# Loading, turning and projecting the first row tile ahead of its chunk in a local-attention and expert-layer kernel

## The chip, the core and the metric

The kernel runs on one core of one Trainium2 chip. The metric is device time in microseconds (us), the median of the runs shown; smaller is better. TensorE is written PE below, VectorE DVE, ScalarE ACT, GpSimd POOL and SyncE SP.

## The reference

There are 4096 rows (2 batches of 2048) of 256 features. The part that the change touches is the attention of the first layer, 16 heads of 16 features, each row seeing itself and the 64 rows before it:

```python
qkv = x @ W_attn + b_attn
q, k, v = jnp.split(qkv, 3, axis=-1)        # 16 heads of 16
scores = jnp.einsum('bhtd,bhsd->bhts', q, k) * scale
mask = causal & (j >= i - 64)
attn = jax.nn.softmax(jnp.where(mask, scores, -jnp.inf), axis=-1)
out = jnp.einsum('bhts,bhsd->bhtd', attn, v)
x1 = layernorm(x + out @ W_proj + b_proj)
...
# then: a router picks one of 8 experts for each row (256 -> 1024, gelu),
# a shared second layer (1024 -> 256), two layernorms
```

## The kernel before

**Tiles, chunks and steps.** A row tile is 128 rows; there are 32, and attention takes one in each step `i` of `for i in range(NT)`. Four tiles make a chunk (`CH` = 512 rows, `TPC` = 4), and there are 8 chunks. The input projection works on whole chunks. A piece of it is named by the triple (chunk, piece, part): piece 0 turns the rows of `xts[c]` by PE transposes into `axT[c]`, with features on the partitions; piece 1 makes the queries, piece 2 the keys, piece 3 the values. Each piece has two parts. `project` issues a part's PE work into a PSUM tile of the pool `ps_m` (tag `pm`, two buffers in turn), and `keep` copies it out and thereby frees the buffer. A part of piece 1 or 2 is two fp32 products of 512 columns, which the profile shows as four PE instructions; a part of piece 3 is eight instructions of 256 columns in two halves.

**What copies what.** In `keep`, part 0 of the turned rows goes by ACT, part 1 by DVE. Part 0 of the queries is copied twice, by ACT (L468) and then by DVE (L476), since two variants of the queries are stored; part 1 twice by DVE (L473, L476). Part 0 of the keys goes by ACT (L482), part 1 by DVE (L487). Values go by DVE (L492) and then by DMAs into the shifted copy `vh` (L503 to L513).

**Before the loop.** SP's queue issues the loads in order: the first chunk's rows (512 KB), the bias rows `bst`, three column blocks of `wa` (queries, keys, values; 256 KB each), and smaller ones; then the second chunk's rows. While they land, PE runs 16 transposes (L391), and DVE and POOL make masks and constants. Then pieces 0, 1 and 2 of chunk 0 are projected and kept, part by part.

**Step 0** is written out by hand: the scores of tile 0 (masks L526, 64 small products L538), four row maxima on DVE (L550), two of the four groups of exponentials on ACT (`exps`, L554), then the parts (0,3,0), (0,3,1), (1,0,0), (1,0,1) projected and kept, then the other two groups of exponentials, and then (1,1,0) and (1,1,1), the second chunk's queries.

**Later steps** run four tiles in different stages: scores of tile `i`, transposes of the probabilities of `i-1` (L609, copied by ACT L615 and DVE L617), `weigh` (L629), normalisation and output projection (`join`, L660) of the tile before, and layernorm of the one before that. `scores(i)` writes four PSUM banks `s0` to `s3`, each of which becomes free when the exponentials of that bank in step `i-1` are done. Two slots of each step (`work[i]`) take one part each of the next chunk's projection from a list, `line`. In steps 1 and 3 one part is split into its halves and fills both slots; step 2 has the turning of chunk 2's part 0 and one part from the list.

**Order.** From the first projection on, the engines are in `manual_schedule`: every engine runs its instructions in the order of the program text. What stands ahead of that is ordered by the framework's scheduler. `turned` gives two PSUM banks in turn (pool `ps_t`) for transposed tiles. After the loop come the expert blocks, with products L222 and L242, which the change leaves alone.

Of the kernel before, what the change touches and what calls it, by code (L numbers as in the profile page):

```python
# [10 lines left out]
F32 = mybir.dt.float32  # L11
BF16 = mybir.dt.bfloat16
I32 = mybir.dt.int32
AF = mybir.ActivationFunctionType
ALU = mybir.AluOpType
AX = mybir.AxisListType

P = 128
CTX = 64
HD = 16  # L20
CH = 512
TPC = CH // P
# [11 lines left out]
def kernel(  # L34
# [16 lines left out]
    nc = tc.nc  # L51
    B, T, C = x.shape
    E, _, FF = w1.shape
    KC = C // P
    NH = C // HD
    NT = B * T // P
# [14 lines left out]
    xf = x.rearrange("b t c -> (b t) c")  # L71
# [8 lines left out]
    ident = const.tile([P, P], F32, name="ident")  # L80
# [40 lines left out]
    def turned(name):  # L121

        turns.append(name)
        return ps_t.tile([P, 4, P], F32, tag=f"pt{len(turns) % 2}", name=name)
# [160 lines left out]
    with ExitStack() as att:  # L285
        aw = att.enter_context(tc.tile_pool(name="aw", bufs=1))
        xp = att.enter_context(tc.tile_pool(name="xp", bufs=2))
        p2 = att.enter_context(tc.tile_pool(name="p2", bufs=2))
        small = att.enter_context(tc.tile_pool(name="small", bufs=4))
        def load_x(c):  # L290
            xt = xp.tile([P, TPC, C], F32, tag="xt", name=f"xt_{c}")
            nc.sync.dma_start(
                out=xt, in_=xf[ts(c, CH), :].rearrange("(j p) c -> p j c", p=P)
            )
            return xt

        xts = {0: load_x(0)}
        bst = aw.tile([3 * KC, P], F32, name="bst")
        nc.sync.dma_start(out=bst, in_=b_attn.rearrange("(g p) -> g p", p=P))
        wa = aw.tile([P, KC, 3 * C], F32, name="wa")  # L300
        wav = w_attn.rearrange("(k p) f -> p k f", p=P)
        for n in range(3):
            nc.sync.dma_start(out=wa[:, :, ts(n, C)], in_=wav[:, :, ts(n, C)])
        bv_bc = aw.tile([P, C], F32, name="bv_bc")
        nc.sync.dma_start(out=bv_bc, in_=b_attn[2 * C : 3 * C].partition_broadcast(P))
        wrs = aw.tile([E, C], F32, name="wrs")
# [11 lines left out]
        def load_rest():  # L318
            nc.sync.dma_start(out=wpj, in_=w_proj.rearrange("(k p) f -> p k f", p=P))
            nc.sync.dma_start(out=bp_bc, in_=b_proj.partition_broadcast(P))  # L320
# [20 lines left out]
        half = aw.tile([P, 2], F32, name="half")  # L341
# [52 lines left out]
        bqkv = aw.tile([P, 3 * KC], F32, name="bqkv")  # L394
# [8 lines left out]
        qs, ks, vs, vh, xbs, axT, x1s, x1Ts, pxs = {}, {}, {}, {}, {}, {}, {}, {}, {}  # L403
# [3 lines left out]
        def project(c, piece, part, halves=(0, 1)):  # L407


            if (c, piece, part) not in pxs:  # L410
                pxs[c, piece, part] = psum(f"pj_{c}_{piece}_{part}")
            pm = pxs[c, piece, part]
            if piece == 0:
                for j in range(TPC):
                    nc.tensor.transpose(pm[:, ts(j, P)], xts[c][:, j, ts(part, P)], ident)
            elif piece in (1, 2):
                f = (piece - 1) * KC + part
                for k in halves:
                    nc.tensor.matmul(  # L419
                        pm, lhsT=wa[:, k, ts(f, P)], rhs=axT[c][:, k, :],  # L420
                        start=(k == 0), stop=(k == KC - 1),
                    )
            else:
                for a in halves:
                    for k in range(KC):
                        nc.tensor.matmul(  # L426
                            pm[:, ts(a, C)],
                            lhsT=axT[c][:, k, ts(2 * part + a, P)],
                            rhs=wa[:, k, 2 * C : 3 * C],
                            start=(k == 0), stop=(k == KC - 1),  # L430
                        )
# [23 lines left out]
                if first:  # L455
                    nc.gpsimd.memset(vh[c][0:CTX, 0].rearrange("p m s d -> p (m s d)"), 0.0)

        def keep(c, piece, part, halves=(0, 1)):
            pm = pxs.pop((c, piece, part))
            if piece == 0:  # L460
                if part == 0:
                    nc.scalar.copy(axT[c][:, part, :], pm)
                else:
                    nc.vector.tensor_copy(axT[c][:, part, :], pm)
            elif piece == 1:
                bias = bqkv[:, part : part + 1]
                if part == 0:
                    nc.scalar.activation(  # L468
                        qs[c][:, part, 1, :], pm, AF.Identity,
                        bias=bq1[:, part : part + 1], scale=half[:, 1:2],  # L470
                    )
                else:
                    nc.vector.tensor_scalar(  # L473
                        qs[c][:, part, 1, :], pm, bias, half[:, 1:2], ALU.add, ALU.mult
                    )
                nc.vector.tensor_scalar(  # L476
                    qs[c][:, part, 0, :], pm, bias, half[:, 0:1], ALU.add, ALU.mult
                )
            elif piece == 2:
                f = KC + part  # L480
                if part == 0:
                    nc.scalar.activation(  # L482
                        ks[c][:, part, CTX : CTX + CH], pm, AF.Identity,
                        bias=bqkv[:, f : f + 1], scale=1.0,
                    )
                else:
                    nc.vector.tensor_scalar(  # L487
                        ks[c][:, part, CTX : CTX + CH], pm, bqkv[:, f : f + 1], None, ALU.add
                    )
            else:  # L490
                for a in halves:
                    nc.vector.tensor_tensor(  # L492
                        vs[c][:, 2 * part + a, :, 0::2, :],
                        pm[:, ts(a, C)].rearrange("p (m s d) -> p m s d", s=2, d=HD),
                        bv_bc.rearrange("p (m s d) -> p m s d", s=2, d=HD),
                        ALU.add,
                    )
                if halves[-1] == 0:
                    return
                v, h = vs[c], vh[c]  # L500
                row = "p j m s d -> p j (m s d)"
                if part == 0 and c % (TPB // TPC) > 0:
                    nc.sync.dma_start(  # L503
                        out=h[low, 0].rearrange("p m s d -> p (m s d)"),
                        in_=vs[c - 1][high, TPC - 1].rearrange("p m s d -> p (m s d)"),
                    )
                t0, t1 = 2 * part, 2 * part + 2
                t2 = min(t1 + 1, TPC)
                nc.sync.dma_start(
                    out=h[low, t0 + 1 : t2].rearrange(row),  # L510
                    in_=v[high, t0 : t2 - 1].rearrange(row),
                )
                nc.sync.dma_start(  # L513
                    out=h[high, t0:t1].rearrange(row), in_=v[low, t0:t1].rearrange(row)
                )
# [598 lines left out]
            )  # L1114

        xts[1] = load_x(1)
        for n in range(3):
            prepare(0, n)
            for part in range(2):
                project(0, n, part)  # L1120
                keep(0, n, part)
            if n == 0:
                load_rest()

        def quick_sums(i, r):

# [9 lines left out]
        parts = []  # L1136
        for c in range(1, NT // TPC):
            parts += [(c, n, p) for n in range(1, TPC) for p in range(2)]
            if c > 1:
                parts[-5:-3] = parts[-4], parts[-5]  # L1140
        line = iter(parts[2:])

        def whole():
            return next(line) + ((0, 1),)
# [2 lines left out]
        for i in range(1, NT - 1):  # L1147
            c = i // TPC + (1 if i % TPC == 0 else 2)
            if i % 2 == 0 and c < NT // TPC:
                work[i] = [(c, 0, 0 if i % TPC else 1, (0, 1)), whole()]  # L1150
            elif i == NT - TPC - 4:
                work[i] = [None, whole()]
            elif i in (1, 3) or NT - 6 <= i < NT - 3:
                one = next(line)
                work[i] = [one + ((0,),), one + ((1,),)]
            elif i == NT - 3:
                one = next(line)
                work[i][1], work[i + 1][1] = one + ((0,), True), one + ((1,), True)
            elif i < NT - 3:
                work[i] = [whole(), whole()]  # L1160
# [40 lines left out]
        for i in range(NT):  # L1201
# [10 lines left out]
            if i == 0:  # L1212
                consts = routing_constants()
                for r in range(1, 4):
                    row_max(t, r)
                for r in range(2):
                    exps(t, r)
                for n in ((0, 3), (1, 0), (1, 1)):
                    prepare(*n)
                for part in ((0, 3, 0), (0, 3, 1), (1, 0, 0), (1, 0, 1)):  # L1220
                    project(*part)
                    keep(*part)
                add_bias(0)
                xts[2] = load_x(2)
                for r in range(2, 4):
                    exps(t, r)
                for part in parts[:2]:
                    project(*part)
                    keep(*part)
                for pair in range(2):  # L1230
                    fold(t, pair)
                continue
# [40 lines left out]
            if i >= TPC - 1 and i % TPC in (0, TPC - 1):  # L1273
                c = (i + 1) // TPC
# [302 lines left out]
```

## Time and profile before

| | |
|---|---|
| median of 3 runs | 584.7 us (584.68 to 584.93) |
| the profiled execution | 585.55 us, of which the span of instructions is 583.7 us |
| granted PE clock, mean | 0.992 |
| PE busy | 555.0 us, 95% of the span |
| DVE, ACT, POOL busy | 402.4, 301.6, 408.0 us |
| first small product of the scores (L538) in step 0, 1, 2 | 16.45, 26.97, 35.16 us |
| the same in step 3, 4, 5 | 43.40, 51.40, 59.85 us |

The busy figures are of one execution and run over stages with different limits. A row of a timeline gives start, duration, engine, line, output and inputs, the count of merged instructions, and in brackets the engine's idle time before it with what ended it. "x8" on a product counts instructions, and a product's record holds the time from its issue to its last result, so that neighbours overlap.

### The profile page before, as it was taken

Reading aid. Unit: us, or ns where it says so; the run is one execution under the profiler, and the core shown is the slowest. Engines: PE = TensorE matmul, PEld = TensorE weight load, DVE = VectorE, ACT = ScalarE, POOL = GpSimd, SP = SyncE. Lnnn points to the kernel's source line nnn. Section 1 sums busy time; section 2 is a strip of 40 time slices with the busy share of each in tenths; the row PEclk is TensorE's granted clock in tenths of the full one; section 3 lists DMA queues with packets and bytes.
Section 4 is the critical chain, followed back from the end, with each engine's and each line's share of the span. In section 5 each row is a group of like instructions: output and inputs, shape, how many; then the busy total and the mean of one; then the engine's idle time right before and its main releaser. Section 6 shows DMA issues by size and latency. Waiting matters only on the chain.

```text
span 583.7 us, 18527 instructions
## 1 busy us (share of the span) xinstructions
PE 555.0 (95%) x7312; PEld 452.0 (77%) x7312; DVE 402.4 (69%) x966; ACT 301.6 (52%) x1005; POOL 408.0 (70%) x603
## 2 busy tenths in 40 slices
PE   8999999999999999999898999999999999999990
PEld 5658667676776767766666898999999999999880
DVE  5659788888988889989877567887863332232582
ACT  2487675776758577576765433233335455455100
POOL 5359777677787887868973488887878677652483
PEclk9999999999999999999999999999999999999996
DMA  5201603012030120211334454555555757754010
GB/s 162 86 2 46 177 25 96 21 45 79 11 104 21 46 76 12 56 30 58 90 105 127 165 181 172 182 182 181 181 194 188 261 180 246 252 160 153 19 39 27
DMA packets 35605, 64.79 MB, mean 111 GB/s; under 512 B 8558, under 2 KB 23484, under 8 KB 35516
## 3 DMA queue, kind: packets, MB, share of 16 engines
q1 hardware_dynamic: 32444, 55.19, 29.6%
q0 software_dynamic: 3072, 8.39, 4.5%
q8 instruction: 59, 0.97, 0.7%
q14 instruction: 30, 0.25, 0.1%
HBM read 48.93 MB, written 8.39 MB: 98 GB/s over the span
## 4 chain that ended last, share of the span: by engine, by line
PE 60%; POOL 14%; DVE 10%; ACT 6%; issue 3%; DMA 1%; POOLq 0%; DVEq 0%; ACTq 0%
PE ph L222 16%; PE py L242 14%; PE pt L609 6%; PE pj L419 4%; ACT pr L554 4%; PE pa L629 4%; PE py L660 4%; PE s L538 3%; POOL fd L574 3%; POOL fd L566 2%; PE pj L426 2%; DVE nm L550 2%; POOL row L849 2%; PE s L526 2%; POOL out_dram L274 1%
## 5 line engine op out<-in xcount | busy, mean ns | idle before, releaser
L554 ACT ACTIVATE pr<-s,nm 128x128 f32<-128x128 f32 x512 | 142.2, 416 | 6.9 <-DVE nm L550 5.9
L566 POOL TENSOR_TENSOR fd<-pr 128x512 f32<-128x512 f32 x62 | 79.0, 1274 | 64.6 <-ACT pr L554 64.6
L233 ACT ACTIVATE gT<-ph,bc 128x128 f32<-128x128 f32 x200 | 57.2, 370 | 107.5 <-issue 59.2
L222 PEld LDWEIGHTS ph<-xgT,wb 128*128 128x128 f32 x800 | 93.5, 192 | 1.3
L222 PE MATMUL ph<-xgT,wb 128*128 128x128 f32 x800 | 94.4, 275 | 0.0
L242 PE MATMUL py<-wo_sb,gT 128*128 128x256 f32 x400 | 90.6, 380 | 0.0
L550 DVE TENSOR_REDUCE nm<-s 128x4 f32<-128x512 f32 x128 | 82.0, 680 | 5.8 <-PE s L538 5.5
L574 POOL TENSOR_TENSOR fd<-fd 128x512 f32<-128x512 f32 (+2 forms) x93 | 76.3, 820 | 7.3
L242 PEld LDWEIGHTS py<-wo_sb,gT 128*128 128x128 f32 x400 | 74.1, 190 | 9.0
L609 PE MATMUL pt<-ident,pr 128*128 128x128 f32 x512 | 72.4, 281 | 3.8 <-DVE pT L617 1.6
L615 ACT COPY pT<-pt 128x512 f32<-128x512 f32 x64 | 38.5, 601 | 69.3 <-DVE nm L550 27.3
L609 PEld LDWEIGHTS pt<-ident,pr 128*128 128x128 f32 x512 | 55.4, 141 | 21.3 <-issue 9.7
L419 PE MATMUL pj<-xT,wa 128*128 128x512 f32 x128 | 60.6, 595 | 0.8 <-issue 0.8
L262 DVE TENSOR_TENSOR y<-py,xbo 128x256 f32<-128x256 f32 x32 | 13.5, 422 | 53.3 <-PE py L242 53.3
L617 DVE COPY pT<-pt 128x512 f32<-128x512 f32 x64 | 43.8, 684 | 6.6 <-PE pt L609 6.4
L538 PEld LDWEIGHTS s<-k,q 32*64 32x64 f32 x2048 | 30.8, 130 | 15.6 <-issue 15.0
L222 PE MATMUL ph<-xpT,wb 128*128 128x128 f32 x352 | 40.8, 275 | 0.0
L222 PEld LDWEIGHTS ph<-xpT,wb 128*128 128x128 f32 x352 | 40.1, 192 | 0.1
L538 PE MATMUL s<-k,q 32*64 32x128 f32 x2048 | 38.8, 278 | 0.4 <-DVE k L487 0.4
L272 DVE TENSOR_SCALAR res<-y,mv_c,rs_c 128x256 f32<-128x256 f32 x32 | 16.0, 499 | 28.9 <-POOL rs_c L256 23.9
L419 PEld LDWEIGHTS pj<-xT,wa 128*128 128x128 f32 x128 | 21.7, 190 | 17.6 <-issue 15.5
L255 POOL TENSOR_TENSOR rs_b<-mv_b,eps_ffn 128x1 f32<-128x1 f32 x32 | 9.2, 289 | 37.2 <-DVE mv_b L253 31.5
(235 smaller groups left out, 1005.5 us busy)
## 6 DMA issues: line engine op xcount, KB each, us to landing
wb<-in_L_ffn_W_dram SPq DMA_DIRECT2D x33, 1024.0 KB, 5.1
h<-v SPq DMA_DIRECT2D x24, 192.0 KB, 3.3
xt<-in_L_attn_x_dram SPq DMA_DIRECT2D x8, 512.0 KB, 4.9
x_d<-x SPq DMA_DIRECT2D x32, 128.0 KB, 1.7
wb<-in_L_ffn_W_dram SPq DMA_DIRECT2D x24, 128.0 KB, 2.2
h<-v SPq DMA_DIRECT2D x14, 96.0 KB, 2.7
wo_sb<-in_L_ffn_Wo_dram SPq DMA_DIRECT2D x1, 1024.0 KB
wa<-in_L_attn_W_attn_dram SPq DMA_DIRECT2D x3, 256.0 KB, 5.2
```

Of the source, the lines that this page charges most:

```text
L222: nc.tensor.matmul(phs[b, h][:, f % (NF // 2), :], lhsT=wb[:, k, ts(f, P)], rhs=xT[:, k, :], start=(k == 0), stop=(k == KC - 1),)
L233: nc.scalar.activation(gT[:, f, :], ph[:, f % (NF // 2), :], AF.Gelu, bias=bcs[b][:, f : f + 1], scale=1.0,)
L242: nc.tensor.matmul(py[:, 0:C], lhsT=gT[:, f, :], rhs=wo_sb[:, f, :], start=(f == 0), stop=(f == NF - 1),)
L419: nc.tensor.matmul(pm, lhsT=wa[:, k, ts(f, P)], rhs=axT[c][:, k, :], start=(k == 0), stop=(k == KC - 1),)
L538: nc.tensor.matmul(banks[i][r][a * CTX : (a + 1) * CTX, 2 * g + o, :], lhsT=qs[c][rows, g, o, t0 : t0 + CTX], rhs=ks[c][rows, g, t0 : t0 + P],
L550: nc.vector.tensor_reduce(maxes[i][:, r, :], banks[i][r], AX.X, ALU.max, negate=True)
L554: nc.scalar.activation(probs[i][:, r, x, :], banks[i][r][:, x, :], AF.Exp, bias=maxes[i][:, r, x : x + 1], scale=1.0,)
L566: nc.gpsimd.tensor_tensor(fd[:, 8 * pair : 8 * pair + 8, :], pr[:, two, :, 0:CTX].rearrange("p r x c -> p (r x) c"), pr[:, two, :, CTX:P]. ...
L574: nc.gpsimd.tensor_tensor(fd[:, :, 0:n], fd[:, :, 0:n], fd[:, :, n : 2 * n], ALU.add)
L609: nc.tensor.transpose(pt[:, x, :], probs[i][:, r, x, :], ident)
L615: nc.scalar.copy(pTs[i][:, r], pt)
L617: nc.vector.tensor_copy(pTs[i][:, r], pt)
```

## The change

The first chunk's rows are loaded in two DMAs: tile 0's 128 rows first, the other three tiles' 384 rows after the first two column blocks of `wa`. Before the loop, tile 0 alone is turned (two transposes into one bank of `turned`), copied, and multiplied for queries and keys: four blocks of features by two halves of the contraction, eight products of 128 columns, all into one PSUM bank and in one run; then the six copies out of that bank. The other three tiles of chunk 0 are turned after that. Their queries and keys, (0,1,0), (0,1,1), (0,2,0), (0,2,1), now 384 columns wide, are projected in step 0 behind the scores of tile 0. The second chunk's queries leave step 0 for the list, so that steps 1 and 3 take two whole parts each instead of one in halves.

```diff
-        xts = {0: load_x(0)}
+        xts = {0: xp.tile([P, TPC, C], F32, tag="xt", name="xt_0")}
+        nc.sync.dma_start(out=xts[0][:, 0, :], in_=xf[0:P, :])
         bst = aw.tile([3 * KC, P], F32, name="bst")
         nc.sync.dma_start(out=bst, in_=b_attn.rearrange("(g p) -> g p", p=P))
...
-        for n in range(3):
+        for n in range(2):
             nc.sync.dma_start(out=wa[:, :, ts(n, C)], in_=wav[:, :, ts(n, C)])
+        nc.sync.dma_start(
+            out=xts[0][:, 1:TPC, :], in_=xf[P:CH, :].rearrange("(j p) c -> p j c", p=P)
+        )
+        nc.sync.dma_start(out=wa[:, :, 2 * C : 3 * C], in_=wav[:, :, 2 * C : 3 * C])
...
+            first = 0 if c else 1
             if piece == 0:
-                for j in range(TPC):
+                for j in range(first, TPC):
                     nc.tensor.transpose(pm[:, ts(j, P)], xts[c][:, j, ts(part, P)], ident)
             elif piece in (1, 2):
                 f = (piece - 1) * KC + part
                 for k in halves:
                     nc.tensor.matmul(
-                        pm, lhsT=wa[:, k, ts(f, P)], rhs=axT[c][:, k, :],
+                        pm[:, first * P :], lhsT=wa[:, k, ts(f, P)],
+                        rhs=axT[c][:, k, first * P :],
                         start=(k == 0), stop=(k == KC - 1),
                     )
...
-        def keep(c, piece, part, halves=(0, 1)):
-            pm = pxs.pop((c, piece, part))
+        def keep(c, piece, part, halves=(0, 1), pm=None):
+
+            cols = slice(0, P) if pm is not None else slice(0 if c else P, CH)
+            keys = slice(CTX + cols.start, CTX + cols.stop)
+            if pm is None:
+                pm = pxs.pop((c, piece, part))
+                if piece < 3:
+                    pm = pm[:, cols]
...
         xts[1] = load_x(1)
+        load_rest()
         for n in range(3):
             prepare(0, n)
-            for part in range(2):
-                project(0, n, part)
-                keep(0, n, part)
-            if n == 0:
-                load_rest()
+        px, pq = turned("x_0"), turned("qk_0")
+        for k in range(KC):
+            nc.tensor.transpose(px[:, k, :], xts[0][:, 0, ts(k, P)], ident)
+        for k in range(KC):
+            keep(0, 0, k, pm=px[:, k, :])
+        for f in range(2 * KC):
+            for k in range(KC):
+                nc.tensor.matmul(
+                    pq[:, f, :], lhsT=wa[:, k, ts(f, P)], rhs=axT[0][:, k, 0:P],
+                    start=(k == 0), stop=(k == KC - 1),
+                )
+        for f in range(2 * KC):
+            keep(0, 1 + f // KC, f % KC, pm=pq[:, f, :])
+        for part in range(2):
+            project(0, 0, part)
+            keep(0, 0, part)
...
-        line = iter(parts[2:])
+        line = iter(parts)
...
-            elif i in (1, 3) or NT - 6 <= i < NT - 3:
+            elif NT - 6 <= i < NT - 3:
                 one = next(line)
                 work[i] = [one + ((0,),), one + ((1,),)]
...
-                for n in ((0, 3), (1, 0), (1, 1)):
+                for n in ((0, 3), (1, 0)):
                     prepare(*n)
+                for part in ((0, 1, 0), (0, 1, 1), (0, 2, 0), (0, 2, 1)):
+                    project(*part)
+                    keep(*part)
                 for part in ((0, 3, 0), (0, 3, 1), (1, 0, 0), (1, 0, 1)):
                     project(*part)
                     keep(*part)
...
                 for r in range(2, 4):
                     exps(t, r)
-                for part in parts[:2]:
-                    project(*part)
-                    keep(*part)
                 for pair in range(2):
                     fold(t, pair)
                 continue
```

In `keep`, the copies of pieces 0 to 2 write the columns `cols` (or `keys`) instead of the whole chunk.

More of the change, by code (lines that the diff above doesn't have):

```diff
@@ L456, in prepare @@
                     nc.gpsimd.memset(vh[c][0:CTX, 0].rearrange("p m s d -> p (m s d)"), 0.0)
-        def keep(c, piece, part, halves=(0, 1)):
-            pm = pxs.pop((c, piece, part))
+        def keep(c, piece, part, halves=(0, 1), pm=None):
[5 more added lines that the diff above has]
+                    pm = pm[:, cols]
             if piece == 0:
                 if part == 0:
-                    nc.scalar.copy(axT[c][:, part, :], pm)
+                    nc.scalar.copy(axT[c][:, part, cols], pm)
                 else:
-                    nc.vector.tensor_copy(axT[c][:, part, :], pm)
+                    nc.vector.tensor_copy(axT[c][:, part, cols], pm)
             elif piece == 1:
@@ L468, in keep @@
                     nc.scalar.activation(
-                        qs[c][:, part, 1, :], pm, AF.Identity,
+                        qs[c][:, part, 1, cols], pm, AF.Identity,
                         bias=bq1[:, part : part + 1], scale=half[:, 1:2],
@@ L473, in keep @@
                     nc.vector.tensor_scalar(
-                        qs[c][:, part, 1, :], pm, bias, half[:, 1:2], ALU.add, ALU.mult
+                        qs[c][:, part, 1, cols], pm, bias, half[:, 1:2], ALU.add, ALU.mult
                     )
                 nc.vector.tensor_scalar(
-                    qs[c][:, part, 0, :], pm, bias, half[:, 0:1], ALU.add, ALU.mult
+                    qs[c][:, part, 0, cols], pm, bias, half[:, 0:1], ALU.add, ALU.mult
                 )
@@ L482, in keep @@
                     nc.scalar.activation(
-                        ks[c][:, part, CTX : CTX + CH], pm, AF.Identity,
+                        ks[c][:, part, keys], pm, AF.Identity,
                         bias=bqkv[:, f : f + 1], scale=1.0,
@@ L487, in keep @@
                     nc.vector.tensor_scalar(
-                        ks[c][:, part, CTX : CTX + CH], pm, bqkv[:, f : f + 1], None, ALU.add
+                        ks[c][:, part, keys], pm, bqkv[:, f : f + 1], None, ALU.add
                     )
```

## The prediction

> **What bounds the kernel now.** I read the page's busy line first, then the chain of waits, the times of each step, and the timeline of the first 36 us, where every edit lies.
>
> ```profile
> PE 555.0 (95%) x7312; PEld 452.0 (77%) x7312; DVE 402.4 (69%) x966; ACT 301.6 (52%) x1005; POOL 408.0 (70%) x603
> ```
>
> The average says PE; whether an edit pays depends on the step. The chain from 33.78 us on:
>
> ```profile
> 33.78 1.04 ACT pr L554 x4
> 34.82 0.04 issue
> 34.86 0.37 PE s L526
> 35.23 1.14 PE s L538 x63
> ...
> 44.61 0.22 PE pw L328 x2
> 44.82 1.02 PE pt L609 x8
> 45.85 0.86 PE pj L426 x4
> 46.71 0.87 PE pt L609 x8
> 47.59 0.87 PE pj L426 x4
> 48.45 0.22 PE pr L648 x2
> ```
>
> From step 2 to 77.3 us it is PE without a gap. Just before, step 1 ends on ACT: its exponentials release the last score bank. Busy time from one start of L538 to the next (columns: stretch and length, then PE, PEld, DVE, ACT, POOL, clock, DMA, GB/s):
>
> ```profile
> 16.45:26.97 10.52, 10.02 (x102) 6.29 (x101) 5.84 (x11) 5.62 (x18) 3.64 (x3) 1.00 0.40 116
> 26.97:35.16 8.19, 6.95 (x154) 4.54 (x152) 5.22 (x10) 6.17 (x20) 3.13 (x6) 1.00 0.01 4
> 43.40:51.40 8.00, 8.00 (x168) 6.44 (x166) 6.72 (x16) 5.84 (x20) 7.19 (x11) 1.00 0.16 43
> ```
>
> Step 1 has 1.24 us of PE to spare; step 3 has none. The opening, from the timeline and the list of waits:
>
> ```profile
> 5.49 1.97 PE L415 MATMUL pj<-ident,xt 128*128 128x128 f32 x8
> 6.11 1.25 DVE L400 TENSOR_SCALAR bq<-bqkv,half 128x2 f32<-128x2 f32 x1
> 6.92 0.41 POOL L456 MEMSET h<- 64x384 f32 x1
> 8.29 7.37 PE L419 MATMUL pj<-xT,wa 128*128 128x512 f32 x16 [0.83 <-issue]
> 18.32 2.18 ACT L554 ACTIVATE pr<-s,nm 128x128 f32<-128x128 f32 x8 [3.65 <-DVE nm L550]
> 22.26 2.18 ACT L554 ACTIVATE pr<-s,nm 128x128 f32<-128x128 f32 x8
> ```
>
> ```profile
> DVE q L476 <- ACT q L468: 4.9, 2, 2.9
> ```
>
> See three things. L400, of two elements, holds DVE until 7.36. The second pair of exponential groups starts at 22.26, behind only one copy. And DVE waits for ACT although both only read the same PSUM tile: two engines take a bank in turn.
>
> **The change part by part.**
>
> *Loads.* One DMA more on SP, 0.4 to 0.5 us of issue for everything behind it; the second chunk's rows landed at 11.0 and are wanted at 21, so the slip costs nothing. Tile 0's 128 KB and the first two blocks of `wa` (640 KB with it) replace the first 640 KB of a larger set. Before, those two blocks had landed by 7.12 with 1.05 MB issued; I estimate 6 us. The other 384 rows come behind 640 KB, I estimate 7 to 8 us, wanted after 9. The gain in arrival is not usable: PE runs its 16 transposes until 5.2, and DVE is next.
>
> *Turning tile 0.* Two transposes instead of eight, done at about 6.0; ACT copies the first half by 6.4. DVE's copy of the second half stands behind L400, and L400 behind POOL's memsets, which this change does not move. Row first: L400 takes 1.25 us and ends at 7.36, POOL's last memset at 7.33. [...] I take 7.36; it was hidden before, because the transposes ended at 7.46. A 128-column copy lies between L464's 0.69 us for 512 columns and L329's 0.17 for 16: 0.30. So 7.7.
>
> *The run of products.* Two of its 16 instructions need only ACT's half; 14 remain. The eight early transposes took (1.97 - 0.42)/7 = 0.22 us apart, later ones (21.14 us, 0.60 for four) 0.11: PE ran at half pace until about 7, though the granted clock reads 1.00. At 8.29 the products already went at full pace, 0.43 for 512 columns. [...] Before, PE was busy from 1.68 to 7.46; now it is mostly idle from 6.0 to 7.7, which speaks against the change: 14 x 0.213 = 3.0 us instead of 14 x 0.118 = 1.65 (L222: 94.4 us for 800). No run here shows such a gap. I take 3.0, since the gap falls in the very window before the pace rose, and keep 1.65 as the low end. End 10.9 with the last result's latency.
>
> *Six copies out of one bank.* They start after the last product and go one after another: ACT 0.50, DVE 0.36, 0.36, 0.40, ACT 0.41, DVE 0.35 (L468, L476, L473, L482, L487 less 384 columns at 0.7 to 1 ns each), with five hand-overs of 0.06: 2.7 us, so 13.6. Six transposes (0.7) and the masks (0.9) lie beside that. Scores of tile 0 thus start at 13.6 instead of 16.45: a lead of 2.8 us.
>
> *Step 0 behind the scores.* Before, first exponential 1.87 after the scores: now 15.5. Eight exponentials, 2.0: 17.5. PE has meanwhile done (0,1,0) and (0,1,1), 8 x 0.32 = 2.6 us, and both `pm` buffers are full. The copy of (0,1,0) is queued on ACT behind those exponentials: 0.7, then DVE 0.7: 18.9. Only then can (0,2,0) start, and PE has waited about 1.6 us. (0,2,0) and (0,2,1) 2.6: 21.5. Values 2 x 1.73: 25.0. Transposes of chunk 1 0.5, ACT's copy 0.7: 26.2. Only behind that copy stand exponentials 2 and 3: 2.0, to 28.2. Scores of step 1 need those banks: 28.45 instead of 26.97. The lead of 2.8 has become a loss of **1.5 us**, though 3.4 us of work (the second chunk's queries, 8 x 0.43) left the step.
>
> *Steps 1 to 3.* The queries return as one part more, 1.72 us, in step 1 and in step 3. In step 1 the 1.24 idle and about 0.3 at hand-overs take it; the exponentials set its end as before; I charge 0.1. Step 2 swaps one key part for the other (ACT copies it now): 0.1. Step 3 is PE without a gap: **1.6 us**. It should last about 9.6, as step 5 with two whole parts does (59.85 to 69.34 = 9.5). The copies that come along fit: DVE has 5.22 of 8.19 busy in step 1 (1.1 of it with query copies left over from step 0) and gets three query copies of 0.8, in step 3 a key copy of 0.75 on 6.72; ACT has 6.17 of 8.19 and trades a key copy for a query copy.
>
> Other queues: the DMAs of the values (L509, L513) and behind them the load of chunk 2's rows leave SP about 3.5 us later (it issued at 23.39), land by 34 with the 6.8 us of such a load, and are wanted in step 2 near 39. POOL's second fold of tile 0 (24.52) slips to 28.3; its sums are wanted in step 2. POOL's copy L445 (0.29) moves from step 1 to 2, where POOL has 2.6 us free. If any of these covers failed, it would be step 2's PE that waits. From step 4 on the work is the same, and the chain behind it carries the offset to the end.
>
> Sum: 1.5 + 0.1 + 0.1 + 1.6 = 3.3 us on the profiled execution (585.55: span 583.7 plus 1.85 around it, 0.85 above the median). The median goes from 584.7 to **588.0**.
>
> **The rivals.**
>
> A. *Full clock or DVE free early.* Full clock alone takes 1.35 us off: +1.9 (586.6). DVE free at 6.25 alone takes about 0.85 off (the landing of the key weights holds part): +2.45 (587.15). Both: +1.1 (585.8), inside what counts as no change. [...] Against: the rows above.
>
> B. *Faster: the lead survives.* If step 0 were bound by PE alone, its idle before (0.83 at 8.29, some 0.9 in buffer waits, 0.5 at 22.2, 1.24 in step 1: 3.5) would go, less 0.3 for extra weight loads and the short products: -3.2, 581.5. It decides if ACT's copies of (0,1,0) and (1,0,0) do not hold up the banks, that is if the first eight exponentials end before (0,1,1) does. Against: in the queue order PE is through with (0,1,1) at 17.3 and the copies that free its next buffer end at 18.9, and the copy of (1,0,0) still stands ahead of exponentials 2 and 3. That step 3 has no gap for 1.72 us also speaks against it.
>
> C. *The other rows land late.* Transposes of the three tiles stand ahead of the masks and scores in PE's queue. If 384 rows landed after 13, scores slip by the same amount: +1 to +2 on the sum, 589 to 590. Against: the third `wa` block, behind as many bytes, landed at 8.24.
>
> **How the numbers follow.** A measurement of this kernel can tell about 0.2% (1.2 us) from no change. Forecast +3.3: 0.45. Rival A with one relief: 0.30; with both: 0.12. Rival B: 0.07. Rival C or another slip: 0.06. Faster 0.07; same 0.12 plus a tail of the single reliefs, 0.14; slower 0.79. The range goes from the end with both reliefs less 0.5 to the forecast plus 1.6: 585.3 to 589.6.
>
> **What would show it.** Right: L538 of step 0 at 13 to 14 us, of step 1 at 28 to 29 (before 26.97), of step 2 at 36 to 37, of step 4 at 54 to 55 (before 51.40); L400 still about 1.25 us; first-tile products 0.21 apart; ACT's second eight exponentials starting near 26; PE waiting near 18 for a copy. Wrong: step 1 starting before 27, or step 3 staying near 8.0.

## The result, and the profile after

The changed kernel takes 587.92 us (median of 13 runs, 586.42 to 590.0) against 584.83 us for the kernel before, measured beside it (13 runs, 584.51 to 585.64). The ratio is 1.0052, 95% interval 1.0042 to 1.0061: slower by about 3.1 us. The forecast was 588.0, range 585.3 to 589.6. The profiled execution of the changed kernel was its slowest run: 590.0 us, span 588.3, 4.45 us above the profiled execution of before. About 1.4 us of that difference are not in the difference of the medians (3.1), and the profile must be read with that in mind.

The busy line of the page, then the stretches from one start of the score products (now L552) to the next, for steps 0, 1 and 3 (length, then PE, PEld, DVE, ACT, POOL, granted clock, DMA, GB/s):

```profile
PE 558.4 (95%) x7327; PEld 456.8 (78%) x7328; DVE 403.5 (69%) x971; ACT 302.4 (51%) x1008; POOL 408.6 (69%) x603
```

```profile
12.91:28.07 15.16, 12.34 (x109) 7.99 (x109) 7.86 (x15) 6.22 (x20) 3.21 (x3) 1.00 0.20 49
28.07:37.79 9.72, 9.62 (x157) 6.50 (x156) 6.30 (x10) 6.38 (x20) 5.07 (x6) 0.82 0.16 53
46.31:56.03 9.72, 9.72 (x171) 7.20 (x171) 7.22 (x17) 5.93 (x20) 9.33 (x12) 1.00 0.13 34
```

Step 0 is 4.6 us longer than before and leaves PE 2.8 us idle. Step 3 has PE busy to the last tenth and is 1.7 us longer. Step 1 is 1.5 us longer too, but its clock column reads 0.82 instead of 1.00: that is not work.

The opening, from the timeline:

```profile
5.49 0.69 PE L1136 MATMUL x<-ident,xt 128*128 128x128 f32 x2
6.11 1.25 DVE L406 TENSOR_SCALAR bq<-bqkv,half 128x2 f32<-128x2 f32 x1
6.92 0.41 POOL L464 MEMSET h<- 64x384 f32 x1
6.53 4.26 PE L1141 MATMUL qk<-xT,wa 128*128 128x128 f32 x16 [0.35 <-ACT xT L476]
```

Tile 0 is turned by 6.2 us. Two products run, and the other 14 wait for DVE's copy of tile 0, which ends at 7.35 beside the two-element instruction L406 (L400 before). The products end at 10.8.

The chain of waits goes from the last copies of tile 0 through step 0 as follows:

```profile
12.05 0.33 DVE q L490
12.40 0.38 ACT k L496
12.78 0.14 issue
12.91 1.10 PE s L552 x55
14.04 0.70 DVE nm L564
14.77 2.18 ACT pr L568 x8
16.95 0.57 ACT q L482
17.52 0.03 issue
17.54 0.69 DVE q L490
18.23 0.04 issue
18.28 2.85 PE pj L426 x8
21.12 3.45 PE pj L434 x16
24.58 0.45 PE pj L422 x4
25.05 0.59 ACT xT L476
25.64 2.09 ACT pr L568 x8
27.72 0.04 issue
27.77 0.37 PE s L540
28.14 1.94 PE s L552 x64
```

Read downward: the scores start behind ACT's key copy, the fifth of the six copies. Then come eight exponentials on ACT, then ACT's query copy, DVE's query copy, and only then PE again; later ACT's copy of chunk 1's rows, the other eight exponentials, and only then the scores of step 1. A lead of 3.5 us at the first scores (12.92 against 16.45) has become a loss of 1.1 us (28.07 against 26.97).

### The profile page after: what moved, and what is told of

Same layout as the page of the kernel before. It is cut to its first block, busy times and chain, and to the rows that moved or that the text cites. A ratio compares the mean times of both kernels' runs of the same rounds, so it can differ in the third digit from the quotient of the medians.

```text
span 588.3 us, 18568 instructions
## 1 busy us (share of the span) xinstructions
PE 558.4 (95%) x7327; PEld 456.8 (78%) x7328; DVE 403.5 (69%) x971; ACT 302.4 (51%) x1008; POOL 408.6 (69%) x603
## 4 chain that ended last, share of the span: by engine, by line
PE 63%; POOL 14%; DVE 11%; ACT 6%; issue 3%; DMA 1%; POOLq 0%; DVEq 0%; ACTq 0%
PE ph L222 16%; PE py L242 14%; PE pt L623 7%; PE pj L426 6%; ACT pr L568 5%; PE s L552 4%; PE pa L643 4%; PE py L674 4%; POOL fd L588 3%; PE pj L434 2%; POOL fd L580 2%; DVE nm L564 2%; PE s L540 2%; POOL row L863 2%; POOL out_dram L274 1%
## 5 line engine op out<-in xcount | busy, mean ns | idle before, releaser
L623 PEld LDWEIGHTS pt<-ident,pr 128*128 128x128 f32 x512 | 56.1, 142 | 21.9 <-issue 10.6
L426 PE MATMUL pj<-xT,wa 128*128 128x512 f32 (+1 forms) x128 | 58.7, 581 | 1.4 <-DVE q L490 1.4
L552 PEld LDWEIGHTS s<-k,q 32*64 32x64 f32 x2048 | 31.5, 133 | 15.8 <-issue 15.1
L552 PE MATMUL s<-k,q 32*64 32x128 f32 x2048 | 39.6, 283 | 0.8 <-DVE k L501 0.4
L674 PE MATMUL py<-wpj,av 128*128 128x256 f32 x128 | 33.4, 383 | 1.0 <-ACT x1T L717 0.4
```

What stands on the lines that cost most here:

```text
L426: nc.tensor.matmul(pm[:, first * P :], lhsT=wa[:, k, ts(f, P)], rhs=axT[c][:, k, first * P :], start=(k == 0), stop=(k == KC - 1),)
L552: nc.tensor.matmul(banks[i][r][a * CTX : (a + 1) * CTX, 2 * g + o, :], lhsT=qs[c][rows, g, o, t0 : t0 + CTX], rhs=ks[c][rows, g, t0 : t0 + P],
L623: nc.tensor.transpose(pt[:, x, :], probs[i][:, r, x, :], ident)
L674: nc.tensor.matmul(py[:, 0:C], lhsT=av[:, k, :], rhs=wpj[:, k, :], start=(k == 0), stop=(k == KC - 1),)
```

## The experiments

All times are medians beside runs of the kernel before on the same chip (three chips in all, so ratios compare better than medians). The columns "step" give the start of the first score product of that step in the profiled execution. Step 4 minus 51.40 is the offset with which the unchanged rest of the kernel starts; it stays within 0.15 us up to step 31 in every run. From there to PE's end, nine of the eleven profiles take 0.2 to 0.6 us less than the profile of before, whose execution lies 0.7 us above its median; the changed kernel's first and e3's do not.

| kernel | step 0 | step 1 | step 2 | step 4 | offset | median us | ratio to before, 95% interval |
|---|---|---|---|---|---|---|---|
| before | 16.45 | 26.97 | 35.16 | 51.40 | | 584.8 to 585.2 | |
| changed | 12.92 | 28.07 | 37.79 | 56.03 | +4.6 | 587.92 | 1.0052 (1.0042 to 1.0061) |
| e1 queries back in step 0 | 12.58 | 29.89 | 38.08 | 54.32 | +2.9 | 588.11 | 1.0045 (1.0032 to 1.0058) |
| e2 copies on DVE | 11.38 | 24.56 | 32.76 | 50.99 | -0.4 | 585.31 | 1.0002 (0.9993 to 1.0011) |
| e3 filler on PE | 11.38 | 26.52 | 34.73 | 52.95 | +1.5 | 588.96 | 1.0070 (1.0052 to 1.0087) |
| e4 memsets later | 12.44 | 27.59 | 37.28 | 55.51 | +4.1 | 587.74 | 1.0041 (1.0029 to 1.0053) |
| e5 before, queries out of step 0 | 16.18 | 24.54 | 32.74 | 50.98 | -0.4 | 584.88 | 1.0001 (0.9993 to 1.0010) |
| e6 exponentials earlier | 12.90 | 26.59 | 34.79 | 53.01 | +1.6 | 585.95 | 1.0014 (1.0007 to 1.0022) |
| e7 before, load split alone | 20.14 | 30.65 | 38.83 | 55.08 | +3.7 | 588.71 | 1.0056 (1.0042 to 1.0069) |
| e8 e2, e4 and two banks | 11.84 | 25.02 | 33.23 | 51.45 | +0.0 | 583.29 | 0.9973 (0.9963 to 0.9983) |
| e9 changed, again | 11.38 | 26.58 | 36.20 | 54.42 | +3.0 | 588.58 | 1.0068 (1.0048 to 1.0087) |
| e10 e8 with a filler | 10.33 | 23.52 | 31.73 | 49.94 | -1.5 | 583.84 | 0.9978 (0.9969 to 0.9987) |

**e1: the second chunk's queries back in step 0.**

```diff
-        line = iter(parts)
+        line = iter(parts[2:])
...
-            elif NT - 6 <= i < NT - 3:
+            elif i in (1, 3) or NT - 6 <= i < NT - 3:
...
                 for r in range(2, 4):
                     exps(t, r)
+                for part in parts[:2]:
+                    project(*part)
+                    keep(*part)
```

> The changed kernel with one half undone: the second chunk's queries are back at the end of step 0, steps 1 and 3 take one part in halves again. My theory (the lead at the first scores is lost inside step 0, and step 3 pays 1.7 us because it has no PE gap): step 3 (from its first score product to step 4's) falls from 9.7 to 8.0 us, step 0 grows by about 1 us since part of the 3.45 us of products fills the wait for the exponentials; total 0.5 us below the changed kernel, about +2.5 on before (587.3). Rival, the PE pace alone makes the loss: PE idles less at the end of step 0, so the half-pace stretch in step 1 vanishes and the time falls to within 1 us of before.

Its stretches for steps 0, 1 and 3:

```profile
12.57:29.89 17.32, 15.44 (x117) 9.24 (x117) 9.11 (x17) 6.98 (x21) 5.81 (x4) 1.00 0.25 71
29.89:38.07 8.18, 6.95 (x154) 4.54 (x152) 5.23 (x10) 6.16 (x20) 3.12 (x6) 1.00 0.01 2
46.31:54.32 8.01, 8.01 (x169) 6.45 (x167) 6.72 (x16) 5.85 (x20) 7.18 (x11) 1.00 0.11 30
```

Step 3 is back at 8.0, as expected, and step 0 pays instead, by 2.2 us and not the 1 us expected. The total does not fall. The half-pace stretch in step 1 is gone here, and the kernel is as slow as before it went: pace alone is not the cause. Either place for the queries costs about the same, once PE has been kept waiting in step 0: 2.2 us there, against 1.7 in step 3 and 0.3 in step 2.

**e2: step 0's copies on DVE.**

```diff
+            step0 = pm is None and (c, piece) in ((0, 1), (0, 2), (1, 0))
+            act = part == 0 and not step0
...
-                if part == 0:
+                if act:
                     nc.scalar.copy(axT[c][:, part, cols], pm)
```

(and so for the query and the key copy)

> The changed kernel, but in step 0 the copies that ACT made of (0,1,0), (0,2,0) and (1,0,0) go by DVE, so that ACT runs its 16 exponentials in one stretch. My theory (these copies, queued behind and ahead of the exponentials, turn the lead into a loss): exponentials end near 19 instead of 27.5, the wait of PE at 16.7 to 18.3 shrinks to about 1 us, first score product of step 1 at 25.5 to 26 instead of 28.07; total about 2.3 us below the changed kernel, +0.8 on before (585.6). Rival, the pace of PE: its idle stretches are what matters, they shrink too, but step 1 stays at half pace if the clock falls for the idle at 5.9 to 7.4; then the total stays above 587. Rival, DVE becomes the bound (five more copies of 0.6 behind the maxima): step 1 starts no earlier than 27.5.

```profile
12.51 2.85 PE L426 MATMUL pj<-xT,wa 128*128 128x384 f32 x8
13.23 4.23 ACT L570 ACTIVATE pr<-s,nm 128x128 f32<-128x128 f32 x16 [1.63 <-DVE nm L566]
16.22 2.85 PE L426 MATMUL pj<-xT,wa 128*128 128x384 f32 x8 [0.86 <-DVE q L492]
```

All sixteen exponentials run in one stretch, and PE's wait falls from 1.39 to 0.86 us. The changed kernel has:

```profile
18.28 2.85 PE L426 MATMUL pj<-xT,wa 128*128 128x384 f32 x8 [1.39 <-DVE q L490]
```

Step 0 lasts 13.18 instead of 15.16 us, and the total is 2.6 us below the changed kernel's (2.3 was expected). This one edit gives back nearly the whole loss in the median, although DVE gets more copies, so DVE is not the bound. Of the 4.6 us by which the changed kernel's step 0 is longer than that of before, the order on ACT makes 2.0. The rest is mostly work that was moved there (PE is busy for 11.81 us in e2's step 0 and 10.02 before), which the earlier start has to pay for. Even with the order mended, the earlier start wins nothing that can be measured. Of the 5.0 us between the two profiles' offsets, 2.0 are step 0's length; 1.5 come from products at full pace (first scores at 11.38) and 1.5 from a step 1 without the half-pace stretch (8.20).

**e6: only the order.** ACT keeps its copies, but the second eight exponentials come ahead of the values and of chunk 1's turning.

```diff
+                for r in range(2, 4):
+                    exps(t, r)
                 for part in ((0, 3, 0), (0, 3, 1), (1, 0, 0), (1, 0, 1)):
                     project(*part)
                     keep(*part)
                 add_bias(0)
                 xts[2] = load_x(2)
-                for r in range(2, 4):
-                    exps(t, r)
```

> The changed kernel with the third and fourth group of step 0's exponentials ahead of the values and of chunk 1's turning, instead of behind them; the copies stay on ACT. My theory (half of step 0's loss is that these exponentials wait for chunk 1's copy): they end near 22.7 instead of 27.5, step 1 follows chunk 1's transposes and its first score product comes at 26.4 to 26.8 instead of 28.07; ACT's copy of chunk 1's rows is no later, since the transposes end at 24.9. Total 1.4 us below the changed kernel, or 2.5 to 3 if the half-pace stretch of step 1 goes with the idle before it: 585 to 586.5. Rival, only the copies behind the first eight exponentials count (PE's wait at 16.7 to 18.3): no gain, 587.5 or more.

```profile
12.90:26.59 13.69, 11.81 (x109) 7.90 (x109) 7.60 (x15) 6.19 (x20) 6.58 (x6) 1.00 0.12 31
```

Step 0 is 13.69 us long, 1.5 us less, as expected, and step 1 has no half-pace stretch (8.20). The total is 2.0 us below the changed kernel's. In step 0's length, which is free of the pace of products and of step 1, the two places on ACT can be told apart: 1.5 us for the exponentials behind chunk 1's copy, and another 0.5 for the copies behind the first eight, which e2 moves as well (13.18; PE's wait is still 1.38 here and 0.86 there).

**e5: the queries' move alone**, on the kernel before.

```diff
-        line = iter(parts[2:])
+        line = iter(parts)
...
-            elif i in (1, 3) or NT - 6 <= i < NT - 3:
+            elif NT - 6 <= i < NT - 3:
...
-                for part in parts[:2]:
-                    project(*part)
-                    keep(*part)
```

> The kernel before with one part of the change alone: the second chunk's queries leave step 0, and steps 1 and 3 take two whole parts. My theory (the move costs 1.7 us in step 3, nothing in step 1, and saves in step 0 only until the exponentials release the banks at 24.5): first score product of step 1 at 24.7 instead of 26.97, step 1 as long as before (8.2), step 3 at 9.7 instead of 8.0; offset from step 4 on -0.6, total 584.1 to 584.5. Rival, the move itself is what makes the change slow: step 1 pays as well (9.9) and the total is 1 us or more above before. Rival, PE falls to half pace in step 1, as it did in the changed kernel: step 1 at 9.7 and a total of 585.8.

```profile
16.18:24.54 8.36, 6.93 (x94) 5.05 (x94) 4.59 (x9) 4.84 (x17) 1.55 (x2) 1.00 0.31 81
24.54:32.74 8.20, 8.11 (x157) 5.13 (x157) 6.21 (x10) 6.30 (x20) 5.08 (x6) 1.00 0.22 70
41.25:50.98 9.73, 9.73 (x173) 7.21 (x172) 7.21 (x17) 5.93 (x20) 9.34 (x12) 1.00 0.13 36
```

Step 0 saves 2.2 us and not 3.45, step 1 takes a whole part more at no cost (PE busy 8.11 of 8.20, where it was 6.95 of 8.19), and step 3 pays 1.7. Net offset -0.4 (-0.6 expected), in the median nothing that can be measured. The move by itself is not what made the change slow. Four of its 17 runs, at 586.15 to 586.69 us, have a mean granted clock of 0.988 where the other 13 have 0.990 to 0.992, so the rival's half-pace stretch may occur in some runs; the profile is of one without it.

**e4: POOL's memsets later.**

```diff
-                for n in ((0, 3), (1, 0)):
-                    prepare(*n)
+                prepare(1, 0)
...
                 add_bias(0)
+                prepare(0, 3)
```

(both ahead of the values' projection)

> The changed kernel with POOL's memsets of the values' tiles (0.5 and 0.4 us at 6.5 to 7.3) moved behind the bias sums of chunk 0. Theory that the two-element DVE instruction (1.25 us) waits for POOL's unbroken run: it ends near 6.5 instead of 7.36, DVE's copy of tile 0 and with it the products start 0.6 to 0.85 us earlier, the first scores at 12.1 to 12.3 instead of 12.92, total down by 0.6 to 0.8 us. Rival, it waits for something else (the bias rows, a semaphore): it still ends at 7.3 to 7.4 and nothing moves. A third, that PE's pace rises at a fixed time, would let the earlier products run at half pace to the same end plus a few tenths.

```profile
6.11 0.44 DVE L406 TENSOR_SCALAR bq<-bqkv,half 128x2 f32<-128x2 f32 x1
6.32 0.20 POOL L780 MEMSET oh<- 128x8 bf16 x4
6.51 0.29 DVE L478 COPY xT<-x 128x128 f32<-128x128 f32 x1
```

L406 takes 0.44 us instead of 1.25. It ends at 6.55 and POOL's run of memsets at 6.52; in the changed kernel it is 7.36 and 7.33. The first scores come at 12.44, 0.5 us earlier and not 0.6 to 0.8, with the products still 0.213 apart. The median is down by 0.2, within the spread.

**e7: the split of the load alone**, on the kernel before; the edit is the first two hunks of the change.

> The kernel before with the split of the load alone: tile 0's rows first, the other three tiles' rows behind two column blocks of the weights; all else as before. My theory (arrival is hidden behind the 16 transposes, then behind DVE): PE's turning of the chunk starts within 0.3 us of 5.5, unless the 384 rows are the later ones; they then delay it by at most 1.5 us. Total +0 to +1.5. Rival, the split is worth something by itself: first score product before 16.2 and a total below 584.2.

```profile
5.15 0.33 PE L420 MATMUL pj<-ident,xt 128*128 128x128 f32 x1
7.34 1.13 PE L420 MATMUL pj<-ident,xt 128*128 128x128 f32 x7 [1.86 <-DMA xt<-in_L_attn_x_dram]
9.29 9.19 PE L424 MATMUL pj<-xT,wa 128*128 128x512 f32 x14 [0.83 <-ACT xT L467]
```

A miss: the total is 3.9 us up, not 0 to 1.5. The 384 rows land at 7.34 and hold PE for 1.86 us. The wait itself costs about 1 us at the first products (9.29 against 8.29). The rest is pace: the clock reads 0.51 from 8 to 12 us and 0.64 from 12 to 16, and 14 products of 512 columns take 9.19 us where 16 took 7.37 before. In the changed kernel the landing of these rows is covered, since PE wants those rows at 10.6 only.

**e3: a filler on PE.**

```diff
+        pw = psum("warm2")
+        for n in range(7):
+            nc.tensor.transpose(pw[:, 0:P], ident, ident)
         for f in range(2 * KC):
             for k in range(KC):
                 nc.tensor.matmul(
                     pq[:, f, :], lhsT=wa[:, k, ts(f, P)], rhs=axT[0][:, k, 0:P],
```

> The changed kernel with seven more transposes of the identity on PE between tile 0's two transposes and its products, into a bank that nobody reads, so that PE does not idle from 6.0 to 7.4. Theory that the idle holds PE at half pace: the 14 products that stand 0.213 us apart stand about 0.11 apart, the first scores come 1.2 to 1.4 us earlier (11.6 instead of 12.9), and since step 0 keeps its shape the total falls by 1.2 to 1.4 us: +1.8 on before (586.6). Rival, the pace follows the kind of instruction or a fixed time: the products stay at 0.213 and the first scores come 0.1 to 0.4 us later.

The products stand 0.11 apart and step 1 takes 8.21 us, but this profile can't show that the filler did it: e2, without a filler, has the same step 0 start of 11.38. As a test of the cause it is inconclusive. Its offset from step 4 on is +1.5 only, yet the median is 588.96 (586.6 was expected): in the profile the last 20 us are 2.3 us longer. There POOL stands ahead of an output DMA:

```profile
569.25 0.60 POOL L256 TENSOR_TENSOR rs_b<-rs_b,minus_half 128x1 f32<-128x1 f32 x1
572.26 1.23 POOL L274 DMA_INDIRECT out_dram<-res,s_idx_c  x1 [2.40 <-DVE mv_b L253]
```

What held POOL for these 2.40 us is open. In the profiles of before, the changed kernel, e1, e2 and e4 to e8 no wait behind 560 us is longer than 1.3.

**e9: the changed kernel again**, unedited.

> The changed kernel once more, nothing edited, for a second profiled execution. The first one lay 4.6 us behind before from step 4 on, of which 1.5 us are step 1 at half pace (28.0 to 31.4 us) and 1.5 the products at half pace. [...] Rival, the pace is a fixed consequence of this kernel's idle stretches: the pace rises at 10.6 to 11.0 and falls at 28.0 again, offset 4.5 to 4.7.

```profile
7.43 1.83 PE L1141 MATMUL qk<-xT,wa 128*128 128x128 f32 x14 [0.47 <-DVE xT L478]
```

```profile
11.38:26.58 15.20, 12.39 (x108) 7.99 (x108) 7.86 (x15) 6.20 (x20) 3.95 (x3) 0.99 0.20 51
26.58:36.20 9.62, 9.52 (x157) 6.39 (x157) 6.30 (x10) 6.36 (x20) 5.04 (x6) 0.83 0.16 52
```

The same instructions, the same kernel, but here the 14 products take 1.83 us instead of 3.4, and step 1 again holds a half-pace stretch. Offset +3.0, where the rival had 4.5 to 4.7, and the fall is at about 26.4 and not at 28.0. So the pace of the products differs between these two executions; the queue order does not, and step 0 lasts 15.2 us in both. With ACT's order as it is, step 0 is never below 15.1, in e3 either.

**e8: three cures together**, e2 and e4 and the keys' products in a bank of their own.

```diff
-        px, pq = turned("x_0"), turned("qk_0")
+        px, pq = turned("x_0"), turned("q_0")
...
+        pk = turned("k_0")
+        pq = [pq[:, 0], pq[:, 1], pk[:, 0], pk[:, 1]]
         for f in range(2 * KC):
             for k in range(KC):
                 nc.tensor.matmul(
-                    pq[:, f, :], lhsT=wa[:, k, ts(f, P)], rhs=axT[0][:, k, 0:P],
+                    pq[f], lhsT=wa[:, k, ts(f, P)], rhs=axT[0][:, k, 0:P],
```

> The changed kernel with three cures at once: step 0's copies on DVE (as in e2), the memsets late (as in e4), and the queries' and the keys' products of tile 0 in two PSUM banks instead of one, so that their copies overlap. My theory adds up: against e2 the products start 0.8 us earlier and the copies take 1.0 us less, first score product at 9.6 to 10.4 (with PE at full pace in the products; 11.2 at half), step 1 at 22.8 to 23.6, offset from step 4 on -2 (or -1 at half pace), total 583 to 584. Rival, the banks of the copies don't matter since DVE has five of the six copies and is the bound: offset no better than -1.2, total 584.3 or more.

583.29 us, ratio 0.9973 (0.9963 to 0.9983): faster than both kernels, by 1.5 us against before. Which of the three cures makes how much of that was not separated. The profiled execution took 584.98 (another 584.97; the other seven lie between 582.95 and 583.43), and its products ran at half pace until 10.3:

```profile
6.53 2.08 PE L1145 MATMUL q<-xT,wa 128*128 128x128 f32 x8 [0.35 <-ACT xT L478]
8.40 1.91 PE L1145 MATMUL k<-xT,wa 128*128 128x128 f32 x8
```

From the end of the products (8.40 + 1.91 = 10.31) to the first scores (11.84) it is 1.5 us, where the changed kernel has 2.1 (10.79 to 12.91). The transposes and masks in PE's own queue now fill that time; the copies no longer set it. The total was foretold, the times in the profile were not: for half pace 11.2 was expected at the first scores and an offset of -1 from step 4 on, and they are 11.84 and 0.0.

**e10: e8 with four filler transposes** ahead of the products, as in e3.

> [...] Theory: the executions with half-pace products (two of e8's nine near 585) go, the products stand 0.11 apart from 7 us on; median as in e8 or up to 0.5 lower, 582.8 to 583.3, and no time above 584.2. Rival, the filler delays the first products and the pace is a matter of chance that it does not touch: median 583.3 to 583.8 with some executions still near 585. Second rival: the last stretch of the kernel (POOL's output DMAs) goes wrong as in e3, where POOL's sequencer stood for 2.2 us near the end: 585 or more although the offset from step 4 on is below 0.

```profile
5.96 1.06 PE L1145 MATMUL warm<-ident 128*128 128x128 f32 x4
6.82 1.17 PE L1148 MATMUL q<-xT,wa 128*128 128x128 f32 x8
7.82 1.06 PE L1148 MATMUL k<-xT,wa 128*128 128x128 f32 x8
```

Offset -1.5, the best of all profiles. The median of 583.84 (ratio 0.9978, interval 0.9969 to 0.9987) is no better than e8's, since the two intervals overlap almost wholly, and it misses the 582.8 to 583.3 expected. None of its 11 runs is above 584.45, where two of e8's nine were near 585: too few to show that the filler narrows the spread, and that it lowers the time is not shown either.

## Why the prediction was right, and where only its sum was

*The result.* 588.0 was foretold and 587.92 measured. Part of that closeness is luck, since two terms were off with opposite signs: the lead, 0.7 us larger, and step 1, 1.4 us larger where PE fell to half pace.

*Arrival and L400.* Right. L406 took 1.25 us again, and in e4, with the two longest memsets moved away, 0.44. DVE's copy of tile 0 ended with it, at 7.35, and not 0.3 us behind it (7.7 foretold). No run shows DVE free at 6.25 or the 0.85 us that rival A gives to it: in e4 L406 ended at 6.55, and the first scores came 0.5 us earlier.

*The run of products.* Foretold 0.213 apart with 0.118 as the low end. Both occur: 0.213 in the first profile and in e4, e6 and e8, 0.11 in e2, e3 and e9. That PE's idle ahead of the products makes them take 3.0 us was the author's estimate, and no run shows it: e9 is the same kernel with no less idle there, and its 14 products took 1.83 us. That the first profile fitted the choice was luck.

*Six copies out of one bank.* Right in kind, too dear: 2.3 us from 10.8 to 13.1, against 2.7. And the scores did not wait for all six: they started at 12.91, behind ACT's key copy. So the lead at the scores was 3.5 us, not 2.8.

*Step 0 behind the scores.* The mechanism is shown by the chain, by e2 and by e6. The length from scores to scores was 15.16 (14.85 foretold). The loss at step 1's start was 1.1 us, foretold 1.5.

*Step 3.* 1.7 us, foretold 1.6; e1 and e5 move it out and in.

*Step 1.* This term was mis-sized. The extra part itself costs nothing there, as foretold (8.2 us in e3, e5, e6 with it). But PE fell to half pace in step 1 in the first profile, in e4 and in e9 (clock 0.82, 0.83 and 0.83): 9.6 to 9.7 us, so 1.5 us for which the sum had 0.1. The prediction asked about the clock in the opening only and not about step 1's. The single runs bear the size out. Of the changed kernel's 13 runs, eight have a mean granted clock of 0.987 to 0.989 and a median of 588.5 us, and five have 0.991 or 0.992 and a median of 587.0.

*The sum again.* For the first profile: -3.5 lead, +4.6 in step 0, +1.5 pace in step 1, +0.3 in step 2, +1.7 in step 3: +4.6, the offset measured. Without step 1's pace it is 3.1, the size of the medians' difference, but that is no confirmation: the runs of that median are a mixture. e9 has a lead of 5.1 and the pace term, and also comes to 3.0.

*The rivals.* A was described rightly as to the clock: e3's offset of +1.5 is the case of full pace throughout (+1.9 foretold). It cannot be seen in the median. B fell, by e2 and e6: PE's idle in step 0 is held by ACT. C (late rows) did not occur in the changed kernel, but e7 shows the landing at 7.34 and that it hurts where nothing covers it.

## What to carry to other kernels

A stage that is started earlier only wins if every engine behind it can start earlier too: ask what stands between the early result and the next use on each in-order queue, here two copies among sixteen exponentials. Copies that free a buffer for the bounding engine belong on a queue where nothing long stands ahead of them. In a short prologue ask about PE's pace behind an idle as well as about its length: here half pace in step 1 cost 1.5 us more, in three profiles with 1.4 us of PE idle at step 0's end (first, e4, e9), though not in e3 and e5 with as much, and in none of the four with 0.5 us (e2, e6, e8, e10).

## What the runs showed of the hardware beyond expectation

PE's half pace in step 1 lasted 3.4 us, and its place differed between two executions of one kernel. In the first profile the clock reads 0.50 from 28.11 to 31.52 us. In e9 it reads 0.80 over 24 to 28 us and 0.77 over 28 to 32, which again makes 3.4 us of half pace, from about 26.4 on; in e4, with 0.94 and 0.63, it is 3.4 us too. In e7's opening, with 0.51 over 8 to 12 us and 0.64 over 12 to 16, it is 6.8. The start of the kernel was at half pace though the clock column reads 1.00 there: the 14 products from 7.43 on stand 0.213 us apart in the first profile and 0.11 in e9. Only the later falls show in the column.

The falls in step 1 came behind short gaps. The 3.4 us ahead of the first profile's fall hold 1.43 us of PE idle (24.69 to 28.10, in gaps of 0.5, 0.3 and 0.7 us); from 20 to 28 us PE idles for 1.43 us in e4 and for 1.42 in e9, and in e7 a gap of 1.86 us ends at 7.34. The amount alone did not decide: e3 idles as e9 does (0.50 us from 20 to 24, 0.92 from 24 to 28), and e5 for 1.43 us from 20 to 28, and in both step 1 ran at full pace; nor did a fall come behind the first profile's single gap of 1.39 us (16.89 to 18.28). With step 0's idle cut (e2, e6, e8, e10), PE idles for only 0.5 us from 20 to 28 us, and no profile has the fall. The single runs are mixed: the mean granted clock is at most 0.989 in 12 of the changed kernel's 17 runs, e9's with them, in 3 of e6's 17, and in none of the 34 of e2, e8 and e10; but it is so in all six of e3's as well, whose profile reads 1.00 up to 368 us. That mean does not tell where a fall lies. The share of idle was not varied on purpose, and what decides on a fall was not shown.

A DVE instruction of two elements (L406) took 1.25 us and ended 0.03 us behind an unbroken run of nine POOL memsets; with the two longest moved away it took 0.44 and ended 0.03 us behind the other seven.
